# Two context paths, keys a batch ahead in written order, and five last blocks side by side

## The chip, the cores and the metric

The kernel runs on one core of one Trainium2 chip. The metric is the device time of a run in microseconds (us). A core has five engines with queues of their own: PE (TensorE, matrix products), DVE (VectorE), ACT (ScalarE), POOL (GpSimd) and SP (SyncE, which here issues the transfers). [...] Data lies in DRAM, in SBUF (128 partitions) and in PSUM, the banks into which PE writes.

## The reference

Four layers on x of shape (8, 56, 56, 128), float32. Layers 0 (a deformable convolution and an MLP) and 1 (a whitening) are not touched. Layers 2 and 3 work on t, 8 images of 3136 tokens of 128 channels:

```python
t = t + _L2_attn_ref(_ln_t(t), L2_attn_W_k, ..., L2_attn_W_o)
t = t + _L2_ffn_ref(_ln_t(t), ...)
t = t + _L3_attn_ref(_ln_t(t), L3_attn_w_in, L3_attn_w_out, L3_attn_b_out, L3_attn_ln_w)
t = t + _L3_ffn_ref(_ln_t(t), ...)
```

Layer 2's attention has 8 heads of 16 channels, and queries, keys and values are the same product:

```python
kqv = x @ W_k.T
h = kqv.reshape(B, S, HEADS, D_K).transpose(0, 2, 1, 3)
scores = jnp.einsum('bhqd,bhkd->bhqk', h, h) / jnp.sqrt(jnp.float32(D_K))
attn = jax.nn.softmax(scores, axis=-1)
ctx = jnp.einsum('bhqk,bhkd->bhqd', attn, h)
...
return ctx @ W_o.T
```

Layer 3's attention is linear. The queries are normalised over the 32 channels of a head, the keys over all 25,088 tokens of the eight images; a 32 x 32 context per head stands for the scores:

```python
qkv = jnp.einsum('hwc,oc->hwo', x, w_in).reshape(N, 3, HEADS, DIM_HEAD)
q, k, v = (qkv[:, 0], qkv[:, 1], qkv[:, 2])
q = jax.nn.softmax(q, axis=-1) / np.sqrt(DIM_HEAD)
k = jax.nn.softmax(k, axis=0)
v = v / N
context = jnp.einsum('nhd,nhe->hde', k, v)
out = jnp.einsum('hde,nhd->nhe', context, q)
```

An output product and a normalisation follow. Each feed-forward part is a mixture of 64 experts, where each expert chooses its 8 best tokens of an image.

## The kernel before, in words

Tokens go in tiles of T = 112, four tiles to a group (448 tokens), seven groups to an image. `token_layers` (L2223) runs layers 2 and 3 one stage after the other: the weights' set-up, `attention_keys`, `query_bound`, `attend`, the experts, `context_sums`, `context_weights`, `linear_layer` and the experts again.

`attention_keys` (L1038) takes image after image. It loads the image (two transfers of 56 partitions, in pieces of one token, 512 bytes), stores it in token order (L1062), takes mean and variance of each of the 28 tiles (L1066, L1067, in a helper `rsqrt` the root: DVE at L1139, a POOL power at L1140), normalises (DVE, L112), transposes on PE (L121) and copies to `xT` with ACT (L122). Fourteen products p_h (L1082) give kT, copied out in turn by DVE (L1090) and ACT (L1086), and stored. Twenty-five products p_v (L1097) give the values with a column of ones, copied by ACT (L1105) and DVE (L1107), and stored. Last, POOL squares the values (L1116), and DVE sums and takes the maximum (L1118, L1119): the largest norm of a key bounds the scores, so that attention can subtract one constant in place of a running maximum. `small` says whether that bound is small enough; it chooses between `attend` and `attend_any`. The order of the instructions on each engine is a scheduler's, which goes by costs; an image has two buffers for most tiles and one for kT.

`query_bound` (L2079) does a like thing for layer 3: from the largest norm of a query row of w_in it gives `low3`, the constant to subtract, and `small3`, whether it is below 40. It comes after the keys.

`attend` (L1158) runs in an order written out by hand. Its main loop goes over the steps of scores, exponentials and weighted sums. Transposed exponentials (`sq`) are moved between partitions by POOL copies (L1297) and SP transfers to serve a second block. A block of 384 queries ends with a generator of several parts: load of tokens, product with wo_pad (L1374), sum (L1385), statistics (L1390, L1391, L1392), normalise (L1399), transpose (L1411), copy (L1412), gate product (L1415) and its copy (L1416). `go_on` takes such a generator one part further. When the loop is over, the jobs left take the moved squares in, and the blocks left are finished two at a time. Then the choice of tokens starts with a maximum (L1659) over the image.

`context_sums` (L1944) takes the groups of all images through a pipeline of stages, a new one each turn. A group is normalised (ACT, L2033), transposed, copied (ACT, L122) and stored for later; p_k (L1980) has the keys by channel, 128 x 448. DVE takes their maximum (L1983, L1985), ACT the exponential with its sum (L1992) and the factor by which the old sums fall (L1987); PE transposes the exponentials back (L1997), DVE copies them (L1998), PE sums the products with the normalised tokens (L2002), and DVE adds to the scaled totals (L2004, L2005). `linear_layer` (its exponential is at L2144) uses `low3` if `small3` is set.

Of the kernel before, what the change touches and what calls it, by code (L numbers as in the profile page):

```python
# [8 lines left out]
F32 = mybir.dt.float32  # L9
I32 = mybir.dt.int32  # L10
U32 = mybir.dt.uint32
AF = mybir.ActivationFunctionType
# [6 lines left out]
S = IH * IW  # L19
# [1017 lines left out]

def attention_keys(tc, k, w, yv, tok, kT_out, va_out, low, small):  # L1038

# [3 lines left out]
    nc = tc.nc  # L1043
    n_b = yv.shape[1]
    with ExitStack() as ctx:
        cp = ctx.enter_context(tc.tile_pool(name="akc", bufs=1))
        bp = ctx.enter_context(tc.tile_pool(name="akb", bufs=2))
        ps = ctx.enter_context(tc.tile_pool(name="akp", bufs=6, space=PSUM))
        vas = []
        for i in range(2):  # L1050
# [6 lines left out]
        wk = w.wk.rearrange("p h d -> p (h d)")  # L1057
        for n in range(n_b):
            t_sb = bp.tile([T, NT, C], F32, name="t")
            for h in range(2):  # L1060
                nc.sync.dma_start(t_sb[h * IW : (h + 1) * IW], yv[h, n])
            nc.sync.dma_start(tok[n].rearrange("(t p) c -> p t c", p=T), t_sb)  # L1062
            mv = bp.tile([T, NT, 2], F32, name="mv")
            st = bp.tile([T, NT, 6], F32, name="st")
            for i in range(NT):
                nc.vector.bn_stats(st[:, i], t_sb[:, i])  # L1066
                nc.vector.bn_aggr(mv[:, i], st[:, i])  # L1067
            rs = rsqrt(nc, k, bp, mv, NT)
            xT = bp.tile([C, S], F32, name="xT")
            for g in range(NG):  # L1070
                xn = bp.tile([T, GT, C], F32, name="xn")
                for i in range(GT):
                    normalize(nc, xn[:, i], t_sb[:, g * GT + i], mv, rs, g * GT + i)
                transpose_group(
                    nc, k, ps, "m", xT[:, g * QC : (g + 1) * QC], xn, nc.scalar.copy
                )
            kT = bp.tile([128, 2, S], F32, name="kT", bufs=1)
            for g in range(2):
                for c in range(NG):
                    cols = slice(c * QC, (c + 1) * QC)  # L1080
                    p = ps.tile([128, QC], F32, tag="m", name="p_h")
                    nc.tensor.matmul(  # L1082
                        p, wk[:, g * 128 : (g + 1) * 128], xT[:, cols], start=True, stop=True
                    )
                    if c % 2:
                        nc.scalar.activation(  # L1086
                            kT[:, g, cols], p, AF.Identity, bias=w.one16, scale=DK**-0.25
                        )
                    else:
                        nc.vector.tensor_scalar(  # L1090
                            kT[:, g, cols], p, DK**-0.25, w.one16, ALU.mult, ALU.add
                        )
                nc.sync.dma_start(kT_out[n, g], kT[:, g])
            va = vas[n % 2]
            for t, m in key_tiles():
                p = ps.tile([128, 2, 4, DK], F32, tag="m", name="p_v")
                nc.tensor.matmul(  # L1097
                    p[:m].rearrange("p g j d -> p (g j d)"),
                    xT[:, t * 128 : t * 128 + m],
                    w.wv,  # L1100
                    start=True,
                    stop=True,
                )
                if t % 2:
                    nc.scalar.copy(va[:m, :, t, :, :DK], p[:m])  # L1105
                else:
                    nc.vector.tensor_copy(va[:m, :, t, :, :DK], p[:m])  # L1107
            for g in range(2):
                nc.sync.dma_start(va_out[n, g], va[:, g].rearrange("p t j d -> p (t j d)"))

            sq = bp.tile([128, 2 * KT * 4, DK], F32, name="sq", bufs=1)
            v = va.rearrange("p g t j d -> p (g t j) d")[:, :, :DK]
            nc.gpsimd.tensor_tensor(sq, v, v, ALU.mult)  # L1116
            top = bp.tile([128, 2 * KT * 4], F32, name="top")
            nc.vector.tensor_reduce(top, sq, AX.X, ALU.add)  # L1118
            nc.vector.tensor_reduce(tops[:, n : n + 1], top, AX.X, ALU.max)  # L1119

# [33 lines left out]
def attend(tc, k, w, low, tok, kT_in, va_in, t_out, gate_w, gate_b, taken, pooled):  # L1154
# [11 lines left out]
    with ExitStack() as ctx:  # L1166
# [176 lines left out]
        def finish(n, g, b):  # L1343
# [19 lines left out]
            if g == 0:  # L1363
                return
            t_sb = wp.tile([128, KB + 1, C], F32, name="t", bufs=2)
            for m, i, s in spans:
# [5 lines left out]
            for i, (t, m) in enumerate(tiles):  # L1372
                for h in range(2):
# [6 lines left out]
                    )  # L1380
            st = wp.tile([128, KB + 1, 6], F32, name="st", bufs=2)
            mv = wp.tile([128, KB + 1, 2], F32, name="mv", bufs=2)
            rs = wp.tile([128, KB + 1], F32, name="rs_b", bufs=2)
            for m, i, s in spans:
# [22 lines left out]
            yield True  # L1407
            xT = wp.tile([C, QB + 64], F32, name="xT", bufs=2)
            p = bank([C, 512])
# [19 lines left out]

        ready, ending = [], False  # L1430
        loads = [(u, b) for u in range(1, len(parts)) for b in (8, 7, 3, 2, 1, 6, 5, 4, 0)]
# [19 lines left out]
        for i, (u, b, a, c, m) in enumerate(steps):  # L1451
# [34 lines left out]
            if a < NQ and a != b and c == KB - 1:  # L1486
                move_squares(u, b, a, i)
            reload()
        while jobs:
            keep_squares()  # L1490
            from_squares()
        for work in urgent:
            go_on(work)
        ending = True
        while later:
            for work in later[:2]:
                go_on(work)

# [512 lines left out]


def group_stats(nc, k, pool, x):

# [63 lines left out]

def query_bound(tc, k, w, w_in, low, small):  # L2079


    nc = tc.nc
    with ExitStack() as ctx:
        bp = ctx.enter_context(tc.tile_pool(name="qbb", bufs=1))
        ps = ctx.enter_context(tc.tile_pool(name="qbp", bufs=1, space=PSUM))
        raw = bp.tile([C, C], F32, name="raw")
        nc.sync.dma_start(raw, w_in[:C])
        sq = bp.tile([C, C], F32, name="sq")
        nc.vector.tensor_tensor(sq, raw, raw, ALU.mult)
        norm = bp.tile([C, 1], F32, name="norm")  # L2090
        nc.vector.tensor_reduce(norm, sq, AX.X, ALU.add)
        p = ps.tile([1, C], F32, name="p_n")
# [130 lines left out]
def token_layers(tc, k, a, y, out):  # L2223
# [3 lines left out]
    with ExitStack() as ctx:  # L2227
# [11 lines left out]

        w = Consts()  # L2240
        with tc.tile_pool(name="tlr", bufs=1) as rp:
            with tc.tile_pool(name="tlp", bufs=2, space=PSUM) as ps:
# [34 lines left out]
            small = cp.tile([1, 1], I32, name="small")  # L2277
            attention_keys(tc, k, w, yv, tok, kT_d, va_d, low, small)
        pooled = [cp.tile([C, n_b, E], F32, name=f"pooled{i}") for i in range(2)]
        low3 = cp.tile([128, 1], F32, name="low3")  # L2280
        small3 = cp.tile([1, 1], I32, name="small3")
        query_bound(tc, k, w, a["L3_attn_w_in"], low3, small3)
        dest = (t_a, *gates[0], choices[0], pooled[0])
# [12 lines left out]
        den = mp.tile([C, 1], F32, name="den")  # L2296
        context_sums(tc, k, w, t_a, xT_d, tot, den)
        with tc.tile_pool(name="ex3", bufs=AHEAD) as xp:
# [88 lines left out]
```

## Time and profile before

| | us |
|---|---|
| median of 3 runs | 7568.02 (7562.25 to 7576.92) |
| profiled execution | 7568.32 |
| its span | 7566.5 |
| up to the first normalise of the keys | 1532.7 |
| keys, to attention's first transfer | 336.2 |
| attention, to the last weighted sums | 4528.4 |
| attention's last blocks and the last choice | 80.7 |
| layer 2's experts | 192.0 |
| context sums | 239.3 |
| linear attention and experts of layer 3 | 656.7 |

The stages are cut out of the profiled execution's timeline. A row of the table of stages that the prediction shows has start and end, length, the busy time of each engine with its number of instructions, the granted clock of PE (1 is full), the mean share in which the 16 DMA engines were busy, and GB/s. A row of the timeline has the start, the length from the first to the last of a run of like instructions, the engine and line, out<-in with shapes, the count, and in brackets the idle time before it and what ended that. A row of waits has who waited for whom, the sum in us, the count and the longest. In the whole span PE was busy for 6499.5 us (86%), DVE 5210.3 (69%), ACT 4198.0 (55%) and POOL 2941.4 (39%).

### The profile page before, as it was taken

To read this page: it belongs to the slowest core of one execution; us is meant where nothing else is said; L and a number is where in the kernel's file an instruction comes from. 1 tells how busy PE (TensorE), PEld (TensorE's weight loads), DVE (VectorE), ACT (ScalarE), POOL (GpSimd) and SP (SyncE) were. 2 spreads that over 40 slices of the span, in tenths; PEclk is the share of its full clock that TensorE was granted. 3 is DMA by queue.
4 is the path that set the end of the run, shared out by engine and by line. 5 is a ranking of instruction groups with operands and counts; after the bars stand their busy time and mean duration, and the time that the engine had idled before them with its cause. 6 is when DMAs were issued, how large, how long until landed. Compare 5 with 4: busy or idle time off the path is not lost. (4 is left out here: it accounts for less than half of the span.)

```text
span 7566.5 us, 158564 instructions
## 1 busy us (share of the span) xinstructions
PE 6499.5 (86%) x60063; PEld 2893.4 (38%) x60063; DVE 5210.3 (69%) x9787; ACT 4198.0 (55%) x6563; POOL 2941.4 (39%) x2557
## 2 busy tenths in 40 slices
PE   7859999656999999999999999999999999556764
PEld 5646666433333323323323323323333323245542
DVE  7866664366677777777777777777777777356761
ACT  5634444222766666666666666666666665156750
POOL 0011111122544444444444444444444444333763
PEclk9968989866999999999999999999999999789776
DMA  6544343476888778778778778778778777544544
GB/s 162 163 101 88 85 87 63 155 224 202 198 202 205 188 187 205 190 185 205 192 186 205 189 185 206 187 189 205 191 186 206 187 185 170 202 109 125 134 132 139
DMA packets 737876, 1287.44 MB, mean 170 GB/s; under 512 B 119042, under 2 KB 504452, under 8 KB 730308
## 3 DMA queue, kind: packets, MB, share of 16 engines
q1 hardware_dynamic: 726868, 1260.77, 65.9%
q0 software_dynamic: 6144, 12.60, 0.6%
q8 instruction: 486, 7.96, 0.5%
q10 hardware_dynamic: 4080, 3.68, 0.2%
q14 instruction: 298, 2.44, 0.1%
HBM read 286.04 MB, written 197.81 MB: 64 GB/s over the span
## 5 line engine op out<-in xcount | busy, mean ns | idle before, releaser
L1259 ACT ACTIVATE e<-p_s 128x768 f32<-128x768 f32 (+2 forms) x3712 | 2887.7, 830 | 1577.2 <-PE p_s L1251 1312.7
L1297 POOL COPY x<-sq 32x1152 f32<-32x1152 f32 x1792 | 2062.4, 1151 | 2008.8 <-PE p_s L1251 1240.1
L1270 DVE STREAM_TRANSPOSE sq<-e 128x768 f32<-128x768 f32 x2688 | 2433.8, 950 | 516.7 <-ACT e L1259 267.0
L1251 PE MATMUL p_s<-q,kT 32*128 32x384 f32 (+2 forms) x14848 | 1893.4, 547 | 41.1 <-ACT e L1259 23.3
L1304 PE MATMUL av<-e,va 128*32 128x384 f32 (+2 forms) x14848 | 1644.2, 515 | 13.5 <-DVE acc L1327 8.5
L1304 PE MATMUL avx<-x,va 128*32 128x384 f32 x10752 | 1129.5, 492 | 57.5 <-issue 36.9
L1251 PEld LDWEIGHTS p_s<-q,kT 32*128 32x128 f32 (+1 forms) x14848 | 649.9, 180 | 1265.8 <-issue 836.1
L1304 PEld LDWEIGHTS av<-e,va 128*32 128x32 f32 (+1 forms) x14848 | 293.6, 108 | 1028.7 <-issue 938.6
L1304 PEld LDWEIGHTS avx<-x,va 128*32 128x32 f32 x10752 | 351.8, 111 | 635.8 <-issue 597.4
L616 POOL TENSOR_TENSOR rs<-rs,mhalf 112x4 f32<-112x4 f32 x112 | 116.0, 1036 | 786.2 <-DVE rs L615 786.2
L1323 DVE TENSOR_TENSOR acc<-acc,avx 128x384 f32<-128x384 f32 x336 | 183.7, 547 | 232.3 <-PE avx L1304 227.7
L121 PE MATMUL p_tr<-ident,xn 112*128 112x112 f32 x672 | 132.9, 337 | 184.0 <-DVE xn L112 138.3
L1140 POOL TENSOR_TENSOR rs<-rs,mhalf 112x4 f32<-112x4 f32 (+2 forms) x136 | 167.9, 1235 | 243.6 <-DVE ntop L1985 123.9
L532 ACT COPY wT<-p_w 88x448 f32<-88x448 f32 x152 | 138.1, 923 | 197.8 <-PE p_w L530 159.4
L2033 ACT ACTIVATE xn<-t,ms,rs 112x128 f32<-112x128 f32 x448 | 185.2, 487 | 73.8 <-DVE ms L2026 73.7
L644 PE MATMUL p_f<-x1T,w 128*128 128x448 f32 x448 | 206.1, 584 | 4.4 <-DVE x1T L639 2.8
L121 PEld LDWEIGHTS p_tr<-ident,xn 112*128 112x128 f32 x672 | 97.3, 167 | 278.2 <-issue 184.9
L530 PE MATMUL p_w<-ident,wide 112*88 112x112 f32 x896 | 144.6, 300 | 62.7 <-DMA px<-strips 37.8
L1393 POOL TENSOR_TENSOR rs_b<-rs_b,mhalf 128x3 f32<-128x3 f32 (+1 forms) x72 | 58.5, 815 | 352.8 <-DVE rs_b L1392 350.2
L327 DVE SCALAR_TENSOR_TENSOR acc<-xp,dw,acc 128x3136 f32<-128x3136 f32 x48 | 166.5, 3470 | 37.6 <-ACT acc L322 37.3
L628 DVE TENSOR_TENSOR y<-y,p_rs 128x448 f32<-128x448 f32 x112 | 69.2, 618 | 176.7 <-PE p_rs L621 176.6
L122 ACT COPY xT<-p_tr 128x448 f32<-128x448 f32 x112 | 59.6, 532 | 224.8 <-PE p_tr L121 198.7
(366 smaller groups left out, 7904.0 us busy)
## 6 DMA issues: line engine op xcount, KB each, us to landing
x<-sq SPq DMA_DIRECT2D x5376, 144.0 KB
w<-in_L_ffn_weight_dram SPq DMA_DIRECT2D x64, 1024.0 KB
px<-strips SPq DMA_DIRECT2D x64, 616.0 KB
va_d<-va SPq DMA_DIRECT2D x16, 1600.0 KB
xT_d<-xT SPq DMA_DIRECT2D x112, 224.0 KB
xT<-xT_d SPq DMA_DIRECT2D x112, 224.0 KB
kT_d<-kT SPq DMA_DIRECT2D x16, 1568.0 KB
t<-t_a SPq DMA_DIRECT2D x16, 1568.0 KB
```

The source lines that it names most:

```text
L121: nc.tensor.transpose(p[:, i, :], src[:, i, :], k.ident[:T, :T])
L327: nc.vector.scalar_tensor_tensor(acc, xp[:, j // 3 : j // 3 + IH, j % 3 : j % 3 + IW], dw[:, j : j + 1], acc, ALU.mult, ALU.add,)
L530: nc.tensor.transpose(p[:, g], around[:, :, g], k.ident[:T, :T])
L644: nc.tensor.matmul(p, q.w1[:, f * 128 : (f + 1) * 128], x1T, start=True, stop=True)
L1140: nc.gpsimd.tensor_tensor(rs, rs, k.mhalf[:m, :n], ALU.pow)
L1251: nc.tensor.matmul(ss[j // 2][:m, j % 2, :width], kT[rows, 128 * i : 128 * i + m], q[rows, :width], start=True, stop=True,)
L1259: nc.scalar.activation(e[:m, 2 * j : 2 * j + 2, :width], ss[j][:m, :, :width], AF.Exp)
L1270: nc.vector.transpose(sq[:, :, i, j : j + 2].rearrange("p s j c -> p j s c"), exps[u, b, a, i][:, j : j + 2, :QB].rearrange("p j (s c) -> ...
L1297: nc.gpsimd.tensor_copy(*moves.pop(0))
L1304: nc.tensor.matmul(out, keys[u, b][1][:m, i, j, :], e[j], start=start, stop=stop)
L1323: nc.vector.tensor_tensor(to, to, in_order(av), ALU.add)
L2033: nc.scalar.activation(out[:, i], x[:, i], AF.Identity, bias=ms[:, i : i + 1], scale=rs[:, i : i + 1])
```

## The change

- `attention_keys` now has a written order. A partition holds other tokens: half an image row of 28 tokens, so a load or a store of tokens has 56 partitions with 14,336 contiguous bytes each, and is made in two halves; the store of tokens is cut the same way. `statistics(n + 1)` loads image n + 1 as image n starts, and stores its tokens and takes its statistics between the p_h products of image n. ACT's copy of transposes writes to strided places of `xT`, to have the tokens in order again. All p_h results are copied out by ACT, and kT has two buffers. `largest(n)` issues POOL's squares after image n's values, and DVE's sums and maxima after the normalise of image n + 1.
- `query_bound` becomes `score_bound`, takes key rows too, and goes ahead of the weights' set-up.
- In `attend`, once the main loop is over, all blocks left go on side by side; `room` gives them space in two buffers of squares. Up to there the order is the old one.
- `context_sums_bounded` subtracts the constant `low3` from all keys: no maximum, no scaling. The keys are made by token, 112 x 512, so that their exponentials need no transposes back, and the sums of all groups stay in one PSUM bank, with a column of ones for the denominators. Of a group's four normalisations ACT makes two and DVE two. The old function runs if `small3` is not set.

```diff
-        for n in range(n_b):
+        def statistics(n):
             t_sb = bp.tile([T, NT, C], F32, name="t")
-            for h in range(2):
-                nc.sync.dma_start(t_sb[h * IW : (h + 1) * IW], yv[h, n])
-            nc.sync.dma_start(tok[n].rearrange("(t p) c -> p t c", p=T), t_sb)
+            inner = tok[n].rearrange("(h f i) c -> f h i c", f=2, i=NT)
+            for f in range(2):
+                of = slice(f * IH, (f + 1) * IH)
+                nc.sync.dma_start(t_sb[of], y[:, n, f * NT : (f + 1) * NT])
+            yield
+            for f in range(2):
+                nc.sync.dma_start(inner[f], t_sb[f * IH : (f + 1) * IH])
...
             for i in range(NT):
                 nc.vector.bn_stats(st[:, i], t_sb[:, i])
                 nc.vector.bn_aggr(mv[:, i], st[:, i])
-            rs = rsqrt(nc, k, bp, mv, NT)
+                if i % GT == GT - 1:
+                    yield
+            stats[n] = t_sb, mv, rsqrt(nc, k, bp, mv, NT)
+
+        def largest(n):
+            sq = bp.tile([128, 2 * KT * 4, DK], F32, name="sq", bufs=1)
+            v = vas[n % 2].rearrange("p g t j d -> p (g t j) d")[:, :, :DK]
+            nc.gpsimd.tensor_tensor(sq, v, v, ALU.mult)
+            yield
+            top = bp.tile([128, 2 * KT * 4], F32, name="top")
+            nc.vector.tensor_reduce(top, sq, AX.X, ALU.add)
+            nc.vector.tensor_reduce(tops[:, n : n + 1], top, AX.X, ALU.max)
...
+        for n in range(n_b):
+            t_sb, mv, rs = stats.pop(n)
+            if n + 1 < n_b:
+                ahead.append(statistics(n + 1))
+                advance(ahead)
             xT = bp.tile([C, S], F32, name="xT")
+            by_place = xT.rearrange("c (h f i) -> c i f h", f=2, i=NT)
...
+                nc.scalar.copy(by_place[:, g * GT : (g + 1) * GT], p)
+            advance(tail)
-            kT = bp.tile([128, 2, S], F32, name="kT", bufs=1)
+            kT = bp.tile([128, 2, S], F32, name="kT")
...
-                    if c % 2:
-                        nc.scalar.activation(
-                            kT[:, g, cols], p, AF.Identity, bias=w.one16, scale=DK**-0.25
-                        )
-                    else:
-                        nc.vector.tensor_scalar(
-                            kT[:, g, cols], p, DK**-0.25, w.one16, ALU.mult, ALU.add
-                        )
+                    advance(ahead)
+                    nc.scalar.activation(
+                        kT[:, g, cols], p, AF.Identity, bias=w.one16, scale=DK**-0.25
+                    )
...
+            tail.append(largest(n))
+            advance(tail)
...
-        for work in urgent:
-            go_on(work)
-        ending = True
+            while urgent:
+                go_on(urgent.pop(0))
+        while urgent:
+            go_on(urgent.pop(0))
+        rooms.append(room())
         while later:
-            for work in later[:2]:
-                go_on(work)
+            go_on_all()
...
+def context_sums_bounded(tc, k, w, low, t_in, xT_out, tot, den):
...
+        def group(n, g):
+            if g == 0:
+                load()
+            t = loaded[n][:, g * GT : (g + 1) * GT]
+            rs, mv = group_stats(nc, k, wp, t)
+            yield
+            ms = minus_mean(nc, wp, rs, mv)
+            xn = wp.tile([T, GT, C + 1], F32, name="xn", bufs=6)
+            nc.gpsimd.memset(xn[:, :, C:], 1.0)
+            for i in range(GT):
+                if i % 2:
+                    nc.scalar.activation(xn[:, i, :C], t[:, i], AF.Identity, ...)
+                else:
+                    nc.vector.tensor_scalar(xn[:, i, :C], t[:, i], ...)
+            yield
+            p = ps.tile([C, GT, T], F32, tag="m", name="p_tr")
+            for i in range(GT):
+                nc.tensor.transpose(p[:, i], xn[:, i, :C], k.ident[:T, :T])
+            xT = wp.tile([C, QC], F32, name="xT")
+            nc.scalar.copy(xT, p.rearrange("c a t -> c (a t)"))
+            nc.sync.dma_start(xT_out[n][:, g * QC : (g + 1) * QC], xT)
+            yield
+            p = ps.tile([T, GT, C], F32, tag="m", name="p_k")
+            for i in range(GT):
+                nc.tensor.matmul(p[:, i], xT[:, i * T : (i + 1) * T], w.w_in[:, C : 2 * C], ...)
+            e = wp.tile([T, GT, C], F32, name="e")
+            nc.scalar.activation(e, p, AF.Exp, bias=low[:T])
+            yield
+            for i in range(GT):
+                nc.tensor.matmul(sums, e[:, i], xn[:, i], start=..., stop=...)
...
-def query_bound(tc, k, w, w_in, low, small):
+def score_bound(tc, k, w_in, low, small):
...
-        context_sums(tc, k, w, t_a, xT_d, tot, den)
+        sums = (t_a, xT_d, tot, den)
+        taken = nc.values_load(small3[0:1, 0:1], min_val=0, max_val=1)
+        with tc.If(taken > 0) as both:
+            context_sums_bounded(tc, k, w, low3, *sums)
+        with both.Else():
+            context_sums(tc, k, w, *sums)
```

## The prediction

> **What bounds the kernel now.** I read the table of stages first, then the waits of the keys stage, its timeline, the rates of its transfers, and the timelines of the attention's end and of the context sums. The profiled execution took 7568.3 us, its span 7566.5. Three of seven stages are touched: the keys (from the first normalise), the end of attention, and layer 3's context sums.
>
> ```profile
> core 0: us, PE busy (x) PEld busy (x) DVE busy (x) ACT busy (x) POOL busy (x), PEclk, DMA share, GB/s
> 1532.70:1868.90 336.20, 200.79 (x854) 133.25 (x854) 226.58 (x820) 85.69 (x200) 78.25 (x16) 0.71 0.66 217
> 6397.30:6478.00 80.70, 34.31 (x158) 19.39 (x157) 40.94 (x114) 6.80 (x16) 15.80 (x15) 0.62 0.23 60
> 6670.00:6909.30 239.30, 169.90 (x1008) 122.92 (x1008) 172.26 (x841) 167.47 (x448) 56.40 (x56) 0.95 0.34 96
> ```
>
> No engine is full in any of them (the largest is VectorE, 226.6 of 336 and 172.3 of 239), so waits set them. In the keys stage the waits are a ring:
>
> ```profile
> POOL sq L1116 <- DVE va L1107: 207.0, 8, 26.7
> ACT xT L122 <- PE p_tr L121: 196.9, 56, 33.4
> PE p_tr L121 <- DVE xn L112: 138.3, 8, 28.5
> DVE xn L112 <- POOL rs L1140: 32.4, 8, 5.0
> ```
>
> One image after the other: TensorE stands still some 17 us an image for the normalise, and that waits for statistics, squares and maxima that VectorE does first. Image 3 from its normalise to its last maximum:
>
> ```profile
> 1649.38 4.79 POOL L1140 TENSOR_TENSOR rs<-rs,mhalf 112x28 f32<-112x28 f32 x1 [7.08 <-DVE rs L1139]
> 1654.21 7.27 DVE L112 TENSOR_SCALAR xn<-t,mv,rs 112x128 f32<-112x128 f32 x28 [4.91 <-POOL rs L1140]
> ...
> 1672.65 5.88 PE L1097 MATMUL p_v<-wkT,xT 128*128 128x128 f32 x50
> ...
> 1679.02 5.52 POOL L1116 TENSOR_TENSOR sq<-va 128x3200 f32<-128x3200 f32 x1 [24.85 <-DVE va L1107]
> 1684.57 3.48 DVE L1118 TENSOR_REDUCE top<-sq 128x200 f32<-128x3200 f32 x1 [5.72 <-POOL sq L1116]
> ```
>
> The first normalise starts at 1532.7 for image 0 and about 1828 for image 7: 42.2 us an image.
>
> **Keys: what changes.** Statistics, pow and loads go an image ahead; the squares' maxima go behind the next image's normalise; SP, ACT, DVE, POOL and PE follow a written order; all 14 kT evictions are ACT's. The path of an image, from VectorE's last va copy: normalise, transposes, last copy of xT, 14 matmuls p_h, 25 matmuls p_v, copies.
>
> Here I choose. POOL's squares of the image before (5.5 us) now become ready as the normalise starts, and this trace shows such a meeting twice: a like normalise of attention beside a POOL copy, and alone.
>
> ```profile
> 2345.51 2.60 DVE L1399 TENSOR_SCALAR t<-t,mv,rs_b 128x128 f32<-128x128 f32 x3
> ...
> 2345.70 4.69 POOL L1297 COPY x<-sq 32x1152 f32<-32x1152 f32 x4 [4.62 <-PE p_s L1251]
> ...
> 2449.37 0.82 DVE L1399 TENSOR_SCALAR t<-t,mv,rs_b 128x128 f32<-128x128 f32 x3
> ```
>
> 0.82 becomes 2.60 us. Likewise the 128x128 product of the old query bound took 4.34 us while a square ran on POOL. So I let the squares stop the normalise for their 5.5 us: it ends 12.9 us after the start, not 7.3. Then: PE's last transposes 13.2; the last copy of xT, now strided (0.53 us plain; 1.0 to 1.14 for ACT's strided copies at line 276), 14.3 — the strided layout makes the first p_h wait for all seven copies; 14 p_h at 0.765 us (13 took 9.95) plus a clock still rising, 11.2, to 25.5; p_v 5.9, to 31.4; last copy 31.9. Beside it VectorE does 3.5 + 0.4 of maxima (to 16.8) and 7.3 of statistics (to 24.1), and POOL 4.8 of pow (29.2): hidden by 2.7 us, unless the load comes late. Period 32. ACT's 14 evictions at 0.63 fit under p_h at 0.765; without that cover they would be 8.9 us an image.
>
> Transfers: SP's queue per image is now the va stores of the image before (3.3 MB), load, tok stores (1.6 MB each, waiting for the load to land, with the kT stores queued behind), kT stores (3.2 MB). Long-row stores of 128 partitions run at the first rate, 512-byte rows at the others:
>
> ```profile
> 1634.00:1636.00 2.00, 1.00 0.95 401
> 1650.00:1652.00 2.00, 0.50 0.92 219
> 1652.00:1654.00 2.00, 0.50 0.94 201
> ```
>
> The new load and tok store have rows of 14,336 bytes, but each transfer covers 56 partitions. By the 401 row they cost 4 us each, 24 us of transfers an image. [...] The trace can't decide (its slow rows are short as well as narrow). I take 32 for both; [...].
>
> Sum: first normalise 1529.5 (long-row load 3 us sooner; the moved bound's 128 KB load, seven small VectorE operations and one pow lie in the weights' set-up, between -5 and +6 with it) + 26.1 (image 0, no square pending: 31.9 - 5.6, rounded down for a plain start) + 6 x 32 + 31.6 + 11.9 (last square 5.5, maxima 3.8, the small chain to the bound 2.5) + 1.5 (load of the flag and branch) = 1792.8. Before, attention's first transfer was issued at 1868.9. **Saved 76**; ends 56 (period 35) and 106 (28: no hold-up, then the load-statistics-pow chain sets it). The old bound's 2.3 us after the keys are in it.
>
> **Attention's end.** The last five query blocks ran 2+2+1; a round costs 15 us, mostly latency (wo_pad products at 6410.8, 6429.6, 6444.7), and the choice of tokens starts here:
>
> ```profile
> 6455.02 3.42 DVE L1659 MAX8 best<-pr 64x8 f32<-64x3136 f32 x1
> ```
>
> Side by side they are VectorE's sum: a block is about 4.5 us of it (0.55 + 1.3 + 0.2 + 0.86 + 0.56 + 0.61, with gaps), five are 22, of which some go into the waits for the last two moved squares (6397 to 6411). SP still issues those moves first (busy to 6405.0), then five loads instead of two. I place the first maximum at 6438.5: **saved 16.5**, ends 10 and 20. The 4,460 us of attention before it keep their order on every engine; cost nothing.
>
> **Context sums.** Now one group of four tiles takes 4.25 us, VectorE nearly without a gap; the ring is maximum, exponential, transposes back, copy:
>
> ```profile
> 6792.07 0.61 DVE L1983 TENSOR_REDUCE ntop<-p_k 128x1 f32<-128x448 f32 x1
> ...
> 6793.94 0.16 DVE L2026 SCALAR_TENSOR_TENSOR ms<-mv,rs 112x4 f32<-112x4 f32 x1 [1.07 <-POOL rs L1140]
> ...
> 6796.32 0.61 DVE L1983 TENSOR_REDUCE ntop<-p_k 128x1 f32<-128x448 f32 x1
> ```
>
> Gone per group: VectorE 0.61 + 0.15 + 0.68 + 0.32 + 0.21; ACT 0.29 + 0.19; four transposes. Added: two normalisations moved from ACT (0.48 each) to VectorE (0.26 to 0.34 each), a POOL memset of 112x4 (0.1 to 0.18 by its tiny memsets), one column in each sum. The written order leaves three loops. VectorE with POOL's pow: 2.1 (two ms in a row at the stage's start, where only statistics ran, stood 2.07 apart) + 0.52 + 0.13 = 2.75. PE with ACT: sums 0.97, keys by token 0.97 (the eight matmul rows of p_x), hand-over 0.2, exponential of 112x512 0.69 (the linear layer's), hand-over 0.15: 3.0. ACT alone 2.2. The longest is 3.0. Start 6665.5 instead of 6670.0 (the first statistics no longer stand behind a memset that waited for the scatter); fill 8 + 55 x 3.0 + 1.4 end at 6840; the second branch 0 to 5, taken as 2. Before it ended at 6909.3, minus the 2: about **65 saved**; ends 83 (2.75) and 35 (3.6).
>
> **Total** 76 + 16.5 + 65 = 157.5; 7568.3 - 157.5 = 7410.8. The median of the runs, 7568.0, lies 0.3 from the profiled execution: **7411**, 2.1% less.
>
> **Rivals.** A: squares and normalise don't meet, or pass each other: period 28, 30 us more saved (7 x 4, and 2 at the first and last): 7381. For it: in other places VectorE ran beside POOL undisturbed; against it the two rows above. B: transfers set the keys stage at 35 or a little more, SP standing in front of the tok stores until the load has landed: 24 us less: 7435. [...] against it 401 GB/s. C: the context ring finds another wait (granted clock below the 0.95, or PE's in-order queue held by ACT), 3.7 us a group: 39 less: 7450. D, slower than before: TensorE's granted clock. Attention is 4528 us with PE busy 4364 at a granted 0.98; it decides from 157 us, 3.5% of 4528, so a mean clock below about 0.945 gives 7568 or more, and at 0.94 some 7595. Nothing in the change alters attention's load, so it is remote. E: the bound is refused and both general paths run. Rows of w_in have 128 normal entries over root 128, so a squared norm near 1, at most about 1.4; root of 1.01 x 128 x 1.4 is 13.5 against 40. It would give back 65 and add the general linear layer: about 7480 or more.
>
> **How the numbers follow.** Forecast 0.57, its own range 7395 to 7428 (period 31 to 34, ring 2.8 to 3.2). A 0.14, B 0.13, C 0.12, D 0.02, E 0.01, and 0.01 for a stall I don't see. To hold 8 in 10 the range takes forecast, most of A and B and half of C, with the unknown starts: 7368 to 7460. A measurement tells 0.2%, 15 us, from no change. Faster 0.965; same 0.01 (part of D); slower 0.025.
>
> **What would show it.** Right: the normalise of images 1 to 7 takes some 12.8 us with POOL's square inside it, first normalises 32 apart, p_h starting after the seventh xT copy; the first maximum of the choice 41 after the last av matmul (6398) instead of 57; p_k to p_k 3.0 in the context sums. Wrong: a 7.3 us normalise (A); statistics waiting for the load (B); exponentials waiting long for p_k, or p_k for xT (C); a granted clock under 0.97 in attention (D).

## The result: 7488 us, half of the forecast saving

The changed kernel takes 7488.0 us (median of 4 runs, 7478.0 to 7498.3) against 7566.6 (4 runs, 7562.3 to 7576.9): a ratio of 0.9887, 95% interval 0.9868 to 0.9906. It is 78.6 us faster; 157 were forecast, and 7488 lies above the range of 7368 to 7460. The profiled execution took 7483.6 us with a span of 7481.5, 85.0 us below the span of before; it is one of the two faster runs of the four, so it shows some 6 us more of a saving than the medians do.

Both spans, cut at the same events (the first normalise of the keys, attention's first transfer, the end of the main loop's last weighted sums, `av<-e,va`, the maximum of the last choice, the first statistics of the context sums, the first transpose of their total), show where the time went:

| stage, us | before | after | saved | forecast |
|---|---|---|---|---|
| up to the first normalise | 1532.7 | 1526.0 | 6.7 | 3.2 |
| keys | 336.2 | 279.5 | 56.7 | 73 |
| attention's main loop | 4529.2 | 4538.2 | -9.0 | 0 |
| attention's end | 56.8 | 37.2 | 19.6 | 16.5 |
| choice and layer 2's experts | 215.0 | 215.6 | -0.6 | 4.5, less 2 for the branch |
| context sums | 239.7 | 230.4 | 9.3 | 62.5 |
| rest | 656.8 | 654.5 | 2.3 | 0 |
| span | 7566.5 | 7481.5 | 85.0 | 157.5 |

The forecast column splits the prediction's sum by these stages. The context sums are the miss: 53 of the 72.5 us by which these two profiles fall short of it. The keys are the next, 16.

The table of stages of the changed kernel (start and end, length, busy time of the engines with the number of instructions, granted clock, DMA share, GB/s); its rows are the keys, attention's end, and the context sums:

```profile
core 0: us, PE busy (x) PEld busy (x) DVE busy (x) ACT busy (x) POOL busy (x), PEclk, DMA share, GB/s
1526.00:1805.50 279.50, 211.42 (x851) 137.12 (x851) 225.25 (x749) 151.32 (x264) 77.55 (x15) 0.79 0.72 257
6343.70:6380.90 37.20, 22.73 (x135) 11.99 (x133) 28.45 (x83) 0.00 (x0) 8.56 (x9) 0.84 0.39 101
6596.50:6826.90 230.40, 154.86 (x1120) 133.26 (x1120) 135.24 (x677) 106.92 (x225) 61.36 (x113) 0.95 0.39 110
```

In the context sums VectorE's busy time fell from 172.3 to 135.2 us and ACT's from 167.5 to 106.9, as the change says, and yet the stage is only 9 us shorter: VectorE stood still for 95 us of it, against 67 before. Its largest wait was there before and stayed, the one for POOL's root (waits over 48 groups in the middle of the stage, before and after):

```profile
DVE ms L2026 <- POOL rs L1140: 48.7, 48, 1.4
DVE ms L2174 <- POOL rs L1175: 57.0, 48, 1.2
```

Over the whole stage this wait grew by 12 us, to 66, and some 20 us came in as gaps of 0.03 to 0.11 us, each before an instruction that uses what VectorE has just made. Two groups of tiles on VectorE's timeline show the order; `rs` is what the root is taken of, `ms` minus the mean times the root:

```profile
6700.36 0.17 DVE L1174 TENSOR_SCALAR rs<-mv 112x4 f32<-112x4 f32 x1
6701.72 0.16 DVE L2174 SCALAR_TENSOR_TENSOR ms<-mv,rs 112x4 f32<-112x4 f32 x1 [1.19 <-POOL rs L1175]
6701.99 0.60 DVE L2117 TENSOR_SCALAR xn<-t,rs,ms 112x128 f32<-112x128 f32 x2
6702.51 0.28 DVE L2166 BATCH_NORM_STATS2 st<-t 112x6 f32<-112x128 f32 x1
...
6704.01 0.18 DVE L2167 BATCH_NORM_AGGREGATE mv<-st 112x2 f32<-112x6 f32 x1
6704.30 0.17 DVE L1174 TENSOR_SCALAR rs<-mv 112x4 f32<-112x4 f32 x1
6705.66 0.16 DVE L2174 SCALAR_TENSOR_TENSOR ms<-mv,rs 112x4 f32<-112x4 f32 x1 [1.19 <-POOL rs L1175]
```

From ms to ms 3.94 us. In the written order `rs` of a group is followed on VectorE by `ms` of the same group, which needs POOL's root: VectorE stands still for 1.19 us in every group. A ring (a chain of steps that closes once a group or an image, and so sets the period) of 0.27 to the normalise, 0.52 for it, 1.79 of statistics, 0.32 to POOL's start and 1.04 to the next `ms` makes the 3.94.

The keys' timeline of the changed kernel, from the products of one image to the normalise of the next:

```profile
1637.49 12.67 PE L1126 MATMUL p_h<-xT,wk 128*128 128x448 f32 x28 [1.07 <-ACT xT L1119]
...
1641.26 0.29 DVE L1081 BATCH_NORM_STATS2 st<-t 112x6 f32<-112x128 f32 x1 [1.56 <-DMA t<-y]
...
1652.44 0.18 DVE L1174 TENSOR_SCALAR rs<-mv 112x28 f32<-112x28 f32 x1
...
1652.70 4.80 POOL L1175 TENSOR_TENSOR rs<-rs,mhalf 112x28 f32<-112x28 f32 x1 [23.80 <-DVE rs L1174]
...
1657.46 5.52 POOL L1093 TENSOR_TENSOR sq<-va 128x3200 f32<-128x3200 f32 x1
1657.53 12.46 DVE L112 TENSOR_SCALAR xn<-t,mv,rs 112x128 f32<-112x128 f32 x28 [0.31 <-POOL rs L1175]
```

The normalise takes 12.46 us with POOL's square inside it, as forecast. The period is 34.1 us (the values' stores of images 0 to 6 are issued 33.9 to 34.3 apart), not 32: the statistics take 11.2 us from 1641.26 to `rs`, not 7.3, and they stood waiting for the load. The maximum of the last choice now comes at 6380.94, 37 us after the main loop's last weighted sums:

```profile
6380.94 3.42 DVE L1718 MAX8 best<-pr 64x8 f32<-64x3136 f32 x1
```

### The profile page after: what moved, and what is told of

Same layout as the page of the kernel before. It is cut to its first block, busy times and chain, and to the rows that moved or that the text cites. A ratio compares the mean times of both kernels' runs of the same rounds, so it can differ in the third digit from the quotient of the medians.

```text
span 7481.5 us, 158614 instructions
## 1 busy us (share of the span) xinstructions
PE 6494.3 (87%) x60175; PEld 2906.6 (39%) x60175; DVE 5177.9 (69%) x9559; ACT 4203.2 (56%) x6404; POOL 2949.0 (39%) x2613
## 5 line engine op out<-in xcount | busy, mean ns | idle before, releaser
L1339 PE MATMUL avx<-x,va 128*32 128x384 f32 x10752 | 1129.3, 492 | 60.3 <-issue 33.9
L649 PE MATMUL p_f<-hid,w 128*128 128x448 f32 x448 | 179.8, 544 | 0.0
L645 ACT ACTIVATE hid<-p_f,b 128x448 f32<-128x448 f32 x224 | 137.1, 640 | 54.0 <-PE p_f L644 46.3
L530 PEld LDWEIGHTS p_w<-ident,wide 112*88 112x88 f32 x896 | 118.4, 172 | 110.5 <-issue 77.7
L1360 DVE COPY acc<-avx 128x384 f32<-128x384 f32 x112 | 61.6, 550 | 139.3 <-PE avx L1339 139.3
```

The lines of the kernel that those rows point to most:

```text
L530: nc.tensor.transpose(p[:, g], around[:, :, g], k.ident[:T, :T])
L649: nc.tensor.matmul(p[:, :QC], q.w2[:, f], hid[:, f], start=(f == 0), stop=(f == 3))
L1339: nc.tensor.matmul(out, keys[u, b][1][:m, i, j, :], e[j], start=start, stop=stop)
```

## The experiments

Stage lengths below are cut at the same events as in the table above, each in the run's own profile; "the changed kernel" has keys 279.5, main loop 4538.2, end 37.2, context sums 230.4. All but the first and the last kernel below ran once. Stages that an edit doesn't touch differ from run to run, the keys by up to 4 us, the end by 3, the context sums by 1; the time up to the first normalise lay between 1515 and 1538 (1557 in the run with the slow load), which is why times of single runs are not compared.

### An empty stage before the root is used

```diff
             rs, mv = group_stats(nc, k, wp, t)
             yield
+            yield
             ms = minus_mean(nc, wp, rs, mv)
```

> The changed kernel with one more empty stage between a group's statistics and the use of its root in the bounded context sums; nothing else. The period there is 3.94 us a group. Theory (VectorE waits for POOL's root of the very group whose statistics it has just taken: 1.6 statistics + 0.5 to and in POOL + 1.0 root + 0.2 + 0.6 normalise): the root is covered by the next group's statistics, the period falls to VectorE's sum of 2.7 or PE with ACT's 3.0, so 52 to 70 us less than the changed kernel. Rival (PE's written order with ACT sets the period, as the prediction had it, only larger): 3.9 stays, 0 to 5 us less.

Measured: median 7453.5 us, ratio to before 0.9848 (0.9832 to 0.9865); context sums 188.9, 41.5 less. VectorE's wait for POOL's root is gone (0.4 us in the whole stage), so the theory on the cause holds and the rival falls; the size was short of 52. Over the stage a group takes 3.17 us; where nothing else holds it, this is the ring (all engines' timeline, four rows picked):

```profile
6681.75 1.13 PE L2147 MATMUL sums<-xn,e 112*128 112x129 f32 x8 [0.55 <-ACT e L2144]
...
6682.72 1.04 PE L2136 MATMUL p_k<-w_in,xT 128*112 128x128 f32 x8
...
6683.85 0.69 ACT L2144 ACTIVATE e<-p_k,low 112x512 f32<-112x512 f32 x1 [1.05 <-PE p_tr L2129]
...
6684.69 1.13 PE L2147 MATMUL sums<-xn,e 112*128 112x129 f32 x8 [0.55 <-ACT e L2144]
```

Sums, keys, exponential, sums: 2.94 us, the ring that the prediction had put at 3.0. It was there, behind a longer one. The rest of the 3.17 are pauses, mostly for the stores of xT (ACT waited 11 us in all for them).

### A second empty stage, and statistics apart

```diff
-    for i in range(GT):
-        nc.vector.bn_stats(st[:, i], x[:, i])
-        nc.vector.bn_aggr(mv[:, i], st[:, i])
+    for i in range(GT + 1):
+        if i < GT:
+            nc.vector.bn_stats(st[:, i], x[:, i])
+        if i:
+            nc.vector.bn_aggr(mv[:, i - 1], st[:, i - 1])
...
             nc.scalar.activation(e, p, AF.Exp, bias=low[:T])
             yield
+            yield
```

The empty stage of the first experiment is in it too, and one or two more buffers for tiles that live longer.

> The changed kernel's bounded context sums with a second empty stage, between the exponential and the sums that use it, and with aggregations staggered by one tile (the latter in the linear layer's statistics too). Theory (with one empty stage, sums 0.97 + keys 1.04 + exponential 0.69 + hand-overs 0.24 = 2.94 is a ring of PE and ACT): that ring opens, PE's own sum of 2.6 or VectorE's 2.1 to 2.3 is left, about 2.65 a group, 13 to 18 us less than with one stage, 65 to 72 less than the changed kernel's in this stage. Rival (PE is already full at 2.94 with what the trace models as gaps): no gain over one stage.

Measured: context sums 156.9, 73.5 less than the changed kernel's, 32 less than with one stage (13 to 18 were expected). From the first to the last exponential a group takes 2.61 us. Undisturbed, one exponential follows the other by 2.39 us:

```profile
6641.29 0.69 ACT L2144 ACTIVATE e<-p_k,low 112x512 f32<-112x512 f32 x1 [0.51 <-PE p_tr L2129]
...
6643.68 0.69 ACT L2144 ACTIVATE e<-p_k,low 112x512 f32<-112x512 f32 x1 [0.51 <-PE p_tr L2129]
```

So the expected 2.65 was met by the mean, with its pauses; undisturbed the ring is shorter. The expectation on the gain was too low since it compared with 2.94 undisturbed and not with the 3.17 that one stage really took.

### The keys: three edits, one at a time and together

Statistics apart (as above, in `statistics`):

> The changed kernel with the keys' aggregation of a tile issued after the next tile's statistics, so that no pair stands back to back; nothing else. Theory (a dependent pair costs 0.395 us, apart 0.26; but three chains of nearly the same length close the keys' ring of 34.1 us, and TensorE's, 33, is the next): statistics of an image 11.1 down to 7.3, the period 33, 8 us less in the stage. Rival (VectorE with POOL alone sets the ring): period 30.3, 26 us less. Rival (pairs cost the same): 0.

Measured: statistics 7.5 us instead of 11.2, from the first to `rs`; keys 279.9, nothing gained. The pair does cost 0.26 us apart and 0.395 back to back; the ring hangs on TensorE:

```profile
1611.37 12.53 DVE L112 TENSOR_SCALAR xn<-t,mv,rs 112x128 f32<-112x128 f32 x28
...
1625.48 12.94 PE L1128 MATMUL p_h<-xT,wk 128*128 128x448 f32 x28 [1.07 <-ACT xT L1121]
...
1638.26 2.79 PE L1140 MATMUL p_v<-wkT,xT 128*128 128x128 f32 x20
...
1645.42 5.85 DVE L112 TENSOR_SCALAR xn<-t,mv,rs 112x128 f32<-112x128 f32 x2
```

14.1 to the first product, 12.8 for p_h, 7.2 for p_v and its copies: 34.05, by chance as long as the ring of load, statistics and root, 34.1, in the changed kernel. Expected were 33 and 8 us; TensorE's ring was a microsecond longer.

Squares on ACT:

```diff
-            nc.gpsimd.tensor_tensor(sq, v, v, ALU.mult)
+            nc.scalar.activation(sq, v, AF.Square)
```

> The changed kernel with the squares of the keys' values made by ACT in place of POOL; nothing else. The normalise of images 1 to 7 then takes 7.1 us, not 12.5, in every theory in which POOL's square holds it up; if it stays at 12.5 the hold-up is something else. Theory (the load, landing 17.8 us after the ring's start, with statistics and root behind it, closes the ring just as late): period about 34, stage within 5 us of the changed kernel's. Rival (the hold-up alone sets the ring): period 28.6 to 30, 29 to 38 us less.

```profile
1639.36 7.27 DVE L112 TENSOR_SCALAR xn<-t,mv,rs 112x128 f32<-112x128 f32 x28
...
1639.53 2.87 ACT L1093 ACTIVATE sq<-va 128x3200 f32<-128x3200 f32 x1 [0.48 <-DVE va L1148]
...
1658.32 0.29 DVE L1081 BATCH_NORM_STATS2 st<-t 112x6 f32<-112x128 f32 x1 [7.90 <-DMA t<-y]
...
1669.96 6.36 PE L1138 MATMUL p_v<-wkT,xT 128*128 128x128 f32 x28 [5.49 <-DVE va L1148]
```

The normalise is down to 7.27 us: it was POOL's square that held it, shown. Yet the keys take 285.7 us, 6 more, and 3 more than the longest of the four profiles with these keys untouched (283.1). VectorE now waits 7.9 us for the load, which lands 19 us after the normalise's start; the statistics behind it (11.2) hold up the copies of values that stand after them on VectorE, so PE waits 5.5 us, and its last 28 matmuls of p_v take 6.4 us, where 30 took 3.8 in the changed kernel. The period is 35 to 37 but for the last image. A loss was not expected.

Both of these, with the loads left where they are:

> As the run with three edits, but loads where the changed kernel has them. Theory (the load lands 18.8 us after the values' stores are issued, because 56 partitions move at 200 GB/s behind 3.3 MB of stores): 18.8 + 7.4 + 0.2 + 4.8 = 31.5 a period, stage 18 us shorter than the changed kernel's. Rival (loads are not the limit once VectorE and ACT are free): as the run with three edits.

Measured: keys 253.9, 25.6 less; period 29.9 to 31.0 (31.5 expected). Two edits that gain -6 and 0 alone gain 26 together. With the third:

```diff
+        def load(n):
+            if n >= n_b:
+                return
+            t_sb = bp.tile([T, NT, C], F32, name="t")
+            read[n] = t_sb
+            for f in range(2):
+                of = slice(f * IH, (f + 1) * IH)
+                nc.sync.dma_start(t_sb[of], y[:, n, f * NT : (f + 1) * NT])
...
+            load(n + 2)
             advance(tail)
             kT = bp.tile([128, 2, S], F32, name="kT")
```

> The changed kernel's keys with three edits at once: squares on ACT, aggregations staggered, and the load of image n + 2 issued right after the normalise of image n (its buffer is free then), not at the start of image n + 1. Theory (three rings of 34 us each, so single edits gained nothing): the normalise ends after 7.1 us, nothing waits for a load, and TensorE's ring of last copy 9 to 10, p_h 12.6, p_v 6.9 or the transfers' 29 is left: period 29 to 30, stage 28 to 36 us shorter than the changed kernel's 279.5. Rival (something not seen holds 34): within 5 us.

Measured: keys 239.0, 40.5 less (28 to 36 expected); period 27.8 to 29.6. No wait for a load is left, and the transfers run nearly full, with PE busy for 147 of 160 us:

```profile
1560.00:1720.00 160.00, 147.24 (x571) 91.64 (x571) 124.07 (x567) 115.49 (x188) 27.07 (x6) 0.82 0.92 332
```

So the rival, that something unseen holds 34, falls; the load was worth 15 of the 40.

### Transfers over 112 partitions

The first try put both halves into one transfer:

```diff
-            for f in range(2):
-                of = slice(f * IH, (f + 1) * IH)
-                nc.sync.dma_start(t_sb[of], y[:, n, f * NT : (f + 1) * NT])
+            nc.sync.dma_start(t_sb, y[:, n].rearrange("h (f i) c -> f h i c", f=2))
...
-            for f in range(2):
-                nc.sync.dma_start(inner[f], t_sb[f * IH : (f + 1) * IH])
+            nc.sync.dma_start(inner, t_sb)
```

> The changed kernel with the load and the tok store of an image as one transfer of 112 partitions each, in place of two of 56; rows of 14,336 bytes as before; nothing else. Theory (56 partitions move at about 200 GB/s, whatever the row): the load goes at near 400 GB/s, lands 4 us sooner, VectorE no longer waits 1.5 us for it; the period falls to TensorE's and VectorE's chains, about 33, 7 to 10 us less in the stage. Rival (the rate hangs on the queue or on DRAM): 200 GB/s stays and so does 34.1.

Measured: keys 618.0, 338 more. The theory's 200 GB/s was read from loads of 56 partitions, which ran at 201 to 219 GB/s before, with rows of 512 bytes, and at 201 to 222 in the changed kernel. Three stretches of this run while the load was under way (start and end, length, granted clock, DMA share, GB/s):

```profile
1896.00:1900.00 4.00, 1.00 0.13 54
1900.00:1904.00 4.00, 0.62 0.13 53
1904.00:1908.00 4.00, 0.50 0.12 49
```

A share of 0.13 is what 2 of the 16 engines, busy all the time, would come to (0.125). On the DRAM side the outermost dimension of this transfer is the two halves. The run tells nothing on the number of partitions; it shows 49 to 54 GB/s for a load in this order. What makes it so slow was not tried apart. The second try made the image's row the outermost dimension:

```diff
+            nc.sync.dma_start(t_sb, y[:, n].rearrange("h (f i) c -> h f i c", f=2))
...
+            nc.sync.dma_start(tok[n].rearrange("(p i) c -> p i c", i=NT), t_sb)
...
-            by_place = xT.rearrange("c (h f i) -> c i f h", f=2, i=NT)
+            by_place = xT.rearrange("c (p i) -> c i p", i=NT)
```

> The changed kernel with the partition order (row of the image, half) in place of (half, row): load and tok store of an image are one transfer each over all 112 partitions, [...] rows of 14,336 bytes as before. Theory ([...]): near 400 GB/s over the load, which is over some 4 us sooner. TensorE's ring of 34 with the square in the normalise stays, so the stage gains at most 5 us. Rival (DRAM reads or the first transfer's start hold the rate): 200 to 222 GB/s again.

Measured: keys 280.6, and the load still at 158 to 258 GB/s after the values' stores are through:

```profile
1675.00:1677.00 2.00, 0.50 0.97 410
...
1679.00:1681.00 2.00, 0.50 0.93 258
1681.00:1683.00 2.00, 0.50 0.86 186
1683.00:1685.00 2.00, 0.50 0.88 201
```

In the changed kernel, with two transfers of 56 partitions, the same load and then the tok store look like this:

```profile
1667.00:1669.00 2.00, 0.50 1.03 222
...
1671.00:1673.00 2.00, 0.50 0.95 201
...
1675.00:1677.00 2.00, 0.89 0.93 323
```

So the theory, near 400 GB/s over all partitions, falls for this load: it ran at 158 to 258 GB/s over 112 and at 201 to 222 over 56, while the tok store, in halves of 56 as well, reached 323. What holds this load near 200 GB/s at a DMA share of 0.75 to 0.93, or 0.78 to 1.03 in the changed kernel, is not found. Its rows begin 229,376 bytes apart in DRAM, those of the store 28,672; whether that matters was not tried. It is not loads as such: attention's first loads of keys and values reach 380 GB/s in the changed kernel (1813 to 1817).

### The old end

The attention function of before, in the changed kernel:

> The changed kernel with the attention function of before (last blocks two at a time). Theory: only the end differs, the first maximum of the last choice comes 57 us after the last weighted sums, not 37: 20 us longer, the 4,530 us of the main loop within its own spread of some 10 us. Rival (room, buffer counts or the early rounds also cost something in the main loop, which took 9 us more in the changed kernel's trace): the main loop falls below the changed kernel's by 9 and the net is 11.

Measured: end 56.5, 19.3 us more; main loop 4545.0. The theory holds for the end; the rival falls, since the main loop didn't come back to 4529.

### The old keys, and before once more

> The changed kernel with the keys' function of before; the bound of layer 3 stays ahead of the weights, end and context sums stay changed. The keys' stage, which no longer has the 2.3 us of the old bound behind it, should take 332 to 334 us in place of 279.5. For the open point of attention's main loop (4529 twice in the kernel before, 4530 to 4546 with the new keys): if the new keys' stores or layouts slow it, 4529 comes back; if something else that all these kernels share does (the places in memory behind the bound's early tiles), it stays at 4535 or more; a value between says nothing.

> The kernel before once more, for its stages: attention's main loop took 4529 us in its profile and 4530 to 4546 in nine profiles of kernels with the new keys. Theory (runs of one order of instructions differ by some 15 us there): its main loop lands anywhere from 4525 to 4545, its first normalise from 1515 to 1537. Rival (the new keys cost attention some 9 us): 4529 again, within 2.

Measured: with the old keys, keys 332.6 and main loop 4538.6. Before once more: keys 334.0, main loop 4528.7, end 56.1, context sums 240.1. So two profiles of the kernel before have 4528.7 and 4529.2 in the main loop, as the rival had it, and the twelve of the changed kernel and its variants have 4530.2 to 4546.4, the lowest of them (the run with the slow load) 1 us away. It is not the new keys, since it stays with the old ones, nor the new attention function, since it stays with the old end.

The granted clock has to be read to more digits than the 0.98 that a table gives, since 0.01 of this loop is 45 us. Its mean over the loop, without the first 11 us, was 0.9832 and 0.9817 before and 0.9809 in the changed kernel; the clock withheld adds up to 76 and 83 us before, to 87 in the changed kernel. PE took 4365.3 us in the first profile of before and 4373.2 in the changed kernel for the same 41,555 products. On average the twelve are 10 us longer than the two, with 6.5 us more of clock withheld; the other 3.5 are less than the profiles differ from one another. The run with the slow load, 1 us away, had 77 withheld, and the longest one 95; but the keys with two edits had the least, 73, and were 7 us longer than before. So a slightly lower granted clock fits most of the difference, by comparison and not by an experiment. Why it was lower, and whether the places in memory that the early bound moves matter, was not tried.

### All that gained, together

> The three edits of the keys and the two empty stages with staggered aggregations of the context sums together. Theory (the stages are apart, so gains add): keys 40 and context 73 us below the changed kernel's, median 7488 - 113 = 7375, between 7360 and 7390. Rival (one gain is given back elsewhere, in attention's main loop or the experts' part): above 7395.

Measured: median 7364.5 us (5 runs, 7357.8 to 7377.1), ratio to before 0.9727 (0.9713 to 0.9741), 123.5 us below the changed kernel's median. Keys 238.6, main loop 4535.0, end 37.2, context sums 153.9. The gains of the two stages, 40.9 and 76.5 us here, add, as the stages don't touch each other (40.5 and 73.5 alone).

## Why the prediction was wrong, step by step

**Context sums, the step that failed.** It said: "VectorE with POOL's pow: 2.1 (two ms in a row at the stage's start, where only statistics ran, stood 2.07 apart) + 0.52 + 0.13 = 2.75", and took 3.0 of PE with ACT as the longest loop. VectorE's loop with POOL was 3.94: this term was mis-sized by 1.2 us, and with it the maximum changed hands, 53 us over the stage. Where the 2.07 came from, VectorE's timeline before:

```profile
6673.60 0.15 DVE L1139 TENSOR_SCALAR rs<-mv 112x4 f32<-112x4 f32 x1
6673.66 0.24 DVE L2019 BATCH_NORM_AGGREGATE mv<-st 112x2 f32<-112x6 f32 x2
6673.82 0.26 DVE L2018 BATCH_NORM_STATS2 st<-t 112x6 f32<-112x128 f32 x1
6674.87 0.16 DVE L2026 SCALAR_TENSOR_TENSOR ms<-mv,rs 112x4 f32<-112x4 f32 x1 [0.79 <-POOL rs L1140]
...
6675.67 0.15 DVE L1139 TENSOR_SCALAR rs<-mv 112x4 f32<-112x4 f32 x1
```

The root is in the 2.07, wait and all: 1.27 us from `rs` to `ms`, against 1.36 in the changed kernel. What the scheduler's order had hidden is statistics. Some 0.4 us of them lay inside the root's time, and the pairs went at 0.26 us, none right behind its own statistics, so that only 0.80 us were left from `ms` to the next `rs`. The change writes the order by hand: nothing lies under the root, all four pairs stand between the normalise and `rs`, each 0.395 us instead of 0.26, and they take 1.79 us. Of the 1.87 us between 2.07 and 3.94, the normalise with `ms` is 0.71 (0.65 were forecast), the root 0.09, and the statistics are 1.07, for which nothing was added. The first experiment shows that this loop was the bound, and that the one at 3.0 (2.94) was the next. Rival C named this stage with a period of 3.7, for another wait.

Both, the wait and the pace of the pairs, could be read in the trace of before. The prediction called VectorE "nearly without a gap", but its own row at 6793.94 has VectorE idle for 1.07 us until POOL's root, a quarter of the group's 4.25. And attention's blocks, written by hand already then, have pairs back to back, one every 0.39 us:

```profile
6418.49 0.26 DVE L1390 BATCH_NORM_STATS2 st<-t 128x6 f32<-128x128 f32 x1
6418.78 0.18 DVE L1391 BATCH_NORM_AGGREGATE mv<-st 128x2 f32<-128x6 f32 x1
6418.88 0.26 DVE L1390 BATCH_NORM_STATS2 st<-t 128x6 f32<-128x128 f32 x1
```

**Keys: mechanism right, terms too small.** That POOL's square holds the normalise for 5.5 us was forecast and shown by taking it away (12.5 to 7.3 us). Statistics were put at 7.3 us and "hidden by 2.7 us, unless the load comes late"; they took 11.2, for the same pairs back to back (7.5 with the next tile's statistics between, in the run with statistics apart and in two images before), and the load did come late (1.5 us). p_h was put at 11.2 and took 12.7 to 12.9; p_v with its copies was put at 6.4 and took 7.2. So 32 became 34.1 on two rings at once, 16 us over the stage. For rival A, in the trace of before 231 transposes of 128x768 on VectorE (L1270, 2999 to 3399) took 0.93 to 0.98 us each, with POOL's copies beside some of them and not beside others. Rival B had a period of 35 "or a little more" from transfers, and so had the upper end of the period, by the author's estimate of a load at some 200 GB/s. The load did run at 201 to 222 GB/s, and the DMA share of the stage, 0.66 before, was 0.72; but over all partitions in one transfer it still ran at 158 to 258, so the number of partitions is not shown to be the reason.

**Attention's end** was right: 19.6 us against 16.5, inside 10 to 20, and 19.3 by undoing it.

**The start of the context sums** came as forecast, though the table hides it. First load and first statistics, before and after:

```profile
6655.98 11.95 SPq L1013 DMA_DIRECT2D t<-t_a  x3
...
6670.00 0.49 DVE L2018 BATCH_NORM_STATS2 st<-t 112x6 f32<-112x128 f32 x2
```

```profile
6587.28 11.76 SPq L1013 DMA_DIRECT2D t<-t_a  x3
...
6596.54 0.29 DVE L2166 BATCH_NORM_STATS2 st<-t 112x6 f32<-112x128 f32 x1 [31.61 <-DMA t<-t_a]
```

From the load's issue to the statistics it was 14.0 us and is 9.3, now that the memset no longer stands ahead: 4.8 us, against 4.5. But the load was issued 206.3 us after the last choice's maximum, and 201.0 before. Before once more, which has no branch, had 205.7, and all profiles have 201.0 to 207.8; so the later issue is spread, and the 2 us put down for the branch are not seen.

**The main loop at no cost** was wrong by 9 us in these profiles. Most of it may be the granted clock, which the prediction weighed in rival D for a large loss alone: its mean was lower by 0.002, 11 us more of clock withheld. That is a comparison of traces; the cause stays open.

**The method.** The sum was made of three terms with bounds of their own, but the range was drawn from the likeliest ring in each; the context sums' lower end of 35 rested on a period of 3.6, below what a plain sum of the written order gives. Added one after the other, as the code has them, four pairs at 0.39, `rs` and the way to POOL, its root, the way to `ms` and the normalise come to 1.6 + 0.5 + 1.0 + 0.2 + 0.6, 3.9 us. The stage's own sum was off by a little besides: its terms end at 6839.9, which saves 67 us with the branch and not 65; the ends of 83 and 35 fit the 67.

## What to carry to other kernels

A duration taken from a scheduled kernel holds the overlap that its scheduler made; where a change writes the order out by hand, walk through the new order instruction by instruction, and see what each engine does between asking another for a result and using it. A bracket with a wait in every group, like the 1.07 us here, points to the ring before any change is made. One empty pipeline stage, a word of code, was worth 41 us here, and a second with the statistics apart 32 more. When a stage has several rings of about the same length, single experiments show nothing or even a small loss (0 and -6 us) where the same edits together gain 26, so the rings have to be measured and opened together.

## What the runs showed of the hardware that was not expected

- An aggregation right behind its own statistics on VectorE made a pair 0.395 us (tiles of 112x128); with the next tile's statistics between, 0.26.
- A load with the two halves of the image's rows outermost on the DRAM side ran at a DMA share of 0.12 to 0.15 and 49 to 60 GB/s (48 us of it, 1880 to 1928).
- ACT squared 128 x 3200 strided numbers in 2.87 us, where POOL took 5.52; VectorE's normalise took 12.46 us with POOL's square inside it and 7.27 beside ACT's.
- A load in rows of 14,336 bytes ran at 201 to 222 GB/s in transfers of 56 partitions (DMA share 0.78 to 1.03) and at 158 to 258 in one of 112 (0.75 to 0.93).
